# A planned decoder kernel: triangular inverses started from diagonal blocks of 32 rows instead of 16, with new GpSimd prices for the planner and an earlier load of the second token tile

## The chip, the cores and the metric

The kernel runs on one core of a Trainium2 chip. The metric is device time in microseconds (us) of one execution; lower is better. The kernel before was run three times: 1447.71, 1447.9 and 1452.22 us, median 1447.9 us.

## The reference, cut to what matters

One decoder layer in float32 over 32 sequences of 112 tokens and 256 features: a delta-rule attention block with its own gated MLP, a cross attention with 16 heads over 375 keys, and a mixture of six experts (two per token) plus a shared one. The change lies in the first of these. Its scan is

```python
def step(S, inp):                       # over the 112 tokens of a sequence
    q_t, k_t, v_t, b_t = inp
    Sk = jnp.einsum('bij,bj->bi', S, k_t)
    S = S + b_t[:, None, None] * (v_t - Sk)[:, :, None] * k_t[:, None, :]
    return S, jnp.einsum('bij,bj->bi', S, q_t)
```

Written without the loop, the scan of one sequence is a unit lower triangular system of 112 rows: its strictly lower part holds the products of keys, G = K K^T, with row s scaled by beta_s over the squared norm of key s. The kernel inverts that matrix and multiplies with the result.

## The kernel before, in words

**Groups.** The 32 sequences are worked on in eight groups of four (`GB = 4`), numbered 0 to 7. A group passes through three blocks. `delta_block(g)` and `queries(g)` form a long serial chain. It ends in the tile `qz`, which the group's cross attention needs. The cross attention is cut into 16 "quads" per group (`scores`, `turned`, `product`), each four heads of one sequence. `mixture_sparse(g)` then routes the group's tokens to the experts. The main loop issues the quads of group g one by one and puts between them pieces of the chain of group g + 1 (`main`), pieces of the mixture of group g - 1 (`others`), and the keys and values of the next sequence (`keys_values`). Group 0's chain has no quads to run beside; five steps of group 1's chain and the keys and values of the first two sequences are put into it. When group 7 begins, everything before is flushed, so instructions from either side are not mixed. At the end come 54 tiles of expert work (`sparse_tiles`), the last group's dense mixture, and `combine`, whose 56 row gathers are issued by GpSimd.

**The inverse.** For each of the four matrices of a group, `delta_block` computes G on TensorE, scales it into `W`, writes W to a DRAM table (`low`) and reads back the diagonal blocks of 16 rows, one block per partition (28 of them), as `L`. Forward substitution inverts these blocks: for j = 0 to 14, a product `part` = column j of L times row j of the inverse, and a subtraction from the rows below j. It runs on VectorE in group 0 and on GpSimd in all others (`plain = nc.vector if g == 0 else nc.gpsimd`). The inverted blocks and their transposes go back to two DRAM tables that hold zeros elsewhere, and are read as full 112 x 112 matrices `X` and `Y`. Three levels then double the block size (16 to 32, 32 to 64, 64 to 112). A level masks G (`C`, on GpSimd), multiplies C with X on TensorE (bank `pw`), scales the result to W on VectorE, and multiplies Y with W on TensorE (bank `px`, or `pyt` in the last level), which is subtracted from X. From the second level on Y is made again by transposing X on TensorE (bank `py`) with a copy on ScalarE.

**The order.** All calls go to a `Recorder`, which plans TensorE, VectorE and ScalarE by list scheduling. Each node has a price (`price`) and a number in program order. In the planner's clock, each engine takes the ready node with the lowest number, with a bonus for nodes that read a PSUM bank. A DMA ends a fixed time after its bytes have passed one common queue. The real engines then run in the planned order, each strictly in order, so a wrong price puts an instruction too early or too late in its queue. How many pieces of the chain go between two quads is set by `costs`, one entry for each `yield` of group 0's chain and at least 1.4 us each. PSUM banks (eight) and tile buffers (`qk`, `u`, `vs`, `a`, `G`, `A` exist once; `C` and `W` twice) bound how far work can be pulled forward.

**Names in the profile.** Every planned instruction is sent in line 381 and shows as L381, so tiles tell them apart. The substitution shows as POOL `W<-C,W` (product) and `W<-W` (subtraction); a level's matmuls as PE `X,C`, `W,Y`, `ident,X` and `Y,W`; the attention pieces as `kx,qz`, `ident,e` and `eT,vx`; the chain's MLP as `w_w_gate`, `w_w_up`, `w_w_down`; its last matmul as `w_xwqT`.

Of the kernel before, what the change touches and what calls it, by code (L numbers as in the profile page):

```python
# [15 lines left out]

P = 128
GB = 4
BS = 16
NEG = -1.0e9  # L20
BIG = 3.0e38

# [66 lines left out]
class Recorder:  # L89
# [53 lines left out]
    def price(self, name, op, outs, ins):  # L143
        n = max([self.length(a) for a in outs[:1] + ins] or [1])
        if name == "tensor":
            n = self.length(outs[0])
            return 0.123 if op == "transpose" else 2 * max(0.125, 0.02 + n / 1190)
        if name == "vector":
            if op == "tensor_tensor_reduce":
                return 0.62  # L150
            if op == "tensor_tensor_scan":
                return 0.37
            return max(0.18, 0.05 + n / 800)
        if name == "scalar":
            return 0.15 + n / 1400 + (0.18 if len(outs) > 1 else 0.0)
        if name == "gpsimd":
            return 0.97 if "dma" in op else 0.1 + n / 430
        return 0.08

    def note(self, name, op, args, kwargs):  # L160
# [92 lines left out]
    def flush(self, open_banks=()):  # L253
# [86 lines left out]
        while len(order) < len(nodes):  # L340
            best = None
            for e in self.clock:
                c = candidate(e)
                if c is not None and (best is None or (c[0], c[1].at) < (best[0], best[1].at)):
                    best = c
            if best is None:
                raise RuntimeError("no instruction can be issued")
            start, node = best
            e = node.eng
            for pile in (ready[e], future[e]):  # L350
                for entry in pile:
                    if entry[2] is node:
                        pile.remove(entry)
                        heapq.heapify(pile)
                        break
            node.start = start
            self.clock[e] = start + node.cost
            node.end = self.clock[e]
            if node.lag:
                self.moved = max(self.moved, node.end) + node.lag  # L360
                node.end = self.moved + 1.8
            for key in node.banks:
                self.free.sort()
# [22 lines left out]
def tile_decoder(ctx: ExitStack, tc: tile.TileContext, t: dict, out: bass.AP):  # L386
# [47 lines left out]
    blank = const.tile([T, D], F32, tag="blank", name="blank")  # L434
    nc.vector.memset(blank, 0.0)

    NB = GB * T // BS
    FAR = BS * T + BS
    blocks = [dram.tile([NB, FAR], F32, name=f"blocks_{i}") for i in range(3)]
    kept = [dram.tile([GB, T, D], F32, name=f"kept_{g}") for g in range(groups - 1)]  # L440


# [8 lines left out]


    levels = []
    s = BS
    while s < T:
        n = P // (2 * s)
        lv = const.tile([P, P], F32, tag=f"lv{s}", name=f"lv{s}")
# [26 lines left out]
    nothing = nothing[:T].rearrange("p c n -> p (c n)")[:, : NB * FAR // T]  # L484
    nc.vector.memset(nothing, 0.0)

    unit = const.tile([NB, BS, BS], F32, tag="unit", name="unit")
    nc.gpsimd.memset(unit, 0.0)
    nc.gpsimd.affine_select(
        out=unit, in_=unit, pattern=[[1, BS], [-1, BS]], compare_op=ALU.not_equal, fill=1.0, base=0,  # L490
        channel_multiplier=0,
    )
# [20 lines left out]
    for table in blocks[1:]:  # L513
        nc.gpsimd.dma_start(
            out=table.rearrange("n f -> (n f)").rearrange("(p q) -> p q", p=T), in_=nothing
        )
    nc.gpsimd.dma_start(out=rows[ZERO : ZERO + 1], in_=blank[:1])


# [69 lines left out]
    nc.gpsimd.tensor_tensor(nwb, nwb, wb, ALU.mult)  # L589
    keys_first, mask_first = load_keys(0), load_mask(0)  # L590
    xwk, xwv = weight("xwkT"), weight("xwvT")
    n2 = per_feature("norm2_w")
    wo = weight("Wo")
    w_gate, w_up, w_down = weight("w_gate"), weight("w_up"), weight("w_down")
    xwq, xwo = weight("xwqT"), weight("xwoT")
    keys_second, mask_second = load_keys(1), load_mask(1)
    x_second = load_x(1)
    gb = const.tile([T, NE], F32, tag="gb", name="gb")
    nc.sync.dma_start(out=gb, in_=t["gate_b"].partition_broadcast(T))
    w_route = weight("gate_wT")  # L600
# [92 lines left out]
    def delta_block(g, xt):  # L693
# [79 lines left out]

        W = dlt.tile([T, GB, T], F32, tag="W", name=f"W_{g}", bufs=2)
        plain.tensor_tensor(W, G, bcast(br2, T), ALU.mult)
        low, inv, turned_inv = blocks
        square = lambda m: m.rearrange("(b k) f -> b (k f)", b=GB)[:, : T * T].rearrange(
            "b (s t) -> s b t", s=T
        )
        diagonal = lambda m: m[:, : BS * T].rearrange("n (i t) -> n i t", t=T)[:, :, :BS]  # L780
# [4 lines left out]
        R = dlt.tile([NB, BS * BS + (BS // 2) ** 2], F32, tag="W", name=f"R_{g}", bufs=2)  # L785
        inverse = R[:, : BS * BS].rearrange("p (i j) -> p i j", j=BS)
        plain.tensor_copy(inverse, unit)
        for j in range(BS - 1):
            shape = [NB, BS - 1 - j, j + 1]
            part = R[:, BS * BS : BS * BS + shape[1] * shape[2]].rearrange("p (i j) -> p i j", j=j + 1)  # L790
# [12 lines left out]
        Y = dlt.tile([T, GB, T], F32, tag="Y", name=f"Y_{g}")  # L803
        nc.sync.dma_start(out=X, in_=square(inv))
        nc.sync.dma_start(out=Y, in_=square(turned_inv))
        yield
        yield

# [4 lines left out]
            nc.gpsimd.tensor_tensor(C, G, over_batches(levels[i][:T, :T]), ALU.mult)  # L813
            return C

        C = between_halves(0)
        for i in range(len(levels)):
            pw = bank("pw")
            for b in range(GB):
                matmul(pw[:T, b * T : (b + 1) * T], C[:, b, :], X[:, b, :], start=True, stop=True)  # L820
            W = dlt.tile([T, GB, T], F32, tag="W", name=f"W_{g}_{i}", bufs=2)
            nc.vector.tensor_tensor(W, pw[:T, :NT].rearrange("p (b t) -> p b t", b=GB), bcast(br2, T), ALU.mult)
            if i > 0:
                py = bank("py")
                for b in range(GB):
                    transpose(py[:T, b * T : (b + 1) * T], X[:, b, :], ident[:T, :T])
# [794 lines left out]
```

## Time and profile before

| | |
|---|---|
| median of three runs | 1447.9 us |
| the profiled execution: time, span | 1450.61 us, 1448.9 us |
| TensorE (PE) matmul busy | 1374.7 us, 95% |
| VectorE (DVE) busy | 966.8 us, 67% |
| ScalarE (ACT) busy | 701.3 us, 48% |
| GpSimd (POOL) busy | 305.4 us, 21% |
| mean granted TensorE clock | 0.98 |

A profile line of instructions gives engine, operation, output tile and inputs with their shapes, the count, the busy time, the mean duration of one in ns, and the idle time in front of them with what ended it. In the timeline view the first two columns are start and duration in us, and the bracket at the end is idle time before the instruction. In the view by windows each engine has busy us and a count; the column after POOL is the granted TensorE clock.

### The profile page before, as it was taken

How to read it: one execution, taken by the hardware profiler on the slowest of the kernel's cores; microseconds unless marked ns; L12 is line 12 of the kernel's file. 1: busy time of each engine (PE TensorE's matmuls, PEld its weight loads, DVE VectorE, ACT ScalarE, POOL GpSimd, SP SyncE). 2: the span in 40 equal slices, each digit the busy share in tenths (PEclk: the TensorE clock that was granted, in tenths of full speed). 3: DMA queues.
4: the chain of work that ended last, by engine and by line, in shares of the span. 5: the costliest groups of instructions: out<-in, count | busy, mean ns of one | idle time of the engine just before them, and what ended most of it. 6: DMA issues, size and time to landing. Idle time of an engine off the chain costs nothing.

```text
span 1448.9 us, 26826 instructions
## 1 busy us (share of the span) xinstructions
PE 1374.7 (95%) x9700; PEld 930.0 (64%) x9700; DVE 966.8 (67%) x3171; ACT 701.3 (48%) x1946; POOL 305.4 (21%) x477
## 2 busy tenths in 40 slices
PE   6679999999999989999999899989999999999988
PEld 4456766776577657765676567656766666666654
DVE  6645766865886488648765777577756875464566
ACT  2123756654665366536654565556556664222100
POOL 2121000311031103110311031203120032233175
PEclk9779999999999999999999999999999999999999
DMA  9100100113011301140104101310136022222254
GB/s 282 49 7 13 34 17 17 35 48 112 16 36 48 111 17 36 40 119 16 36 20 126 30 20 33 105 54 19 33 98 179 26 73 66 89 85 88 65 171 146
DMA packets 95076, 94.76 MB, mean 65 GB/s; under 512 B 29920, under 2 KB 89056, under 8 KB 94944
## 3 DMA queue, kind: packets, MB, share of 16 engines
q1 hardware_dynamic: 86816, 72.71, 17.3%
q0 software_dynamic: 8128, 20.34, 4.8%
q8 instruction: 77, 1.26, 0.4%
q14 instruction: 55, 0.45, 0.1%
HBM read 50.90 MB, written 42.12 MB: 64 GB/s over the span
## 4 chain that ended last, share of the span: by engine, by line
PE 67%; DVE 11%; DMA 6%; ACT 5%; POOL 5%; issue 4%; DVEq 0%; SPq 0%; ACTq 0%; POOLq 0%
PE bank L381 57%; PE bank L1327 6%; PE bank L1344 3%; POOL W L381 3%; ACT e L381 3%; DMA blocks<-W 2%; ACT eT L381 1%; DVE e L381 1%; DMA kept<-x 1%; DMA X<-blocks 1%; DVE W L381 1%; DVE mk L381 1%; DVE bst L381 1%; DMA x<-in_x_dram 1%; DVE rs_i L381 1%
## 5 line engine op out<-in xcount | busy, mean ns | idle before, releaser
L381 ACT ACTIVATE e<-e,nmx 112x375 f32<-112x375 f32 x512 | 306.3, 603 | 212.0 <-DVE nmx L381 211.8
L381 DVE CUSTOM_DVE_ANT_0 e<-bank,neg,flip 112x375 f32<-112x375 f32 x512 | 282.6, 603 | 33.7 <-PE bank L381 28.5
L381 ACT COPY eT<-bank 125x448 f32<-125x448 f32 x384 | 184.8, 529 | 86.2 <-PE bank L381 82.8
L381 PEld LDWEIGHTS bank<-ident,e 112*125 112x125 f32 x1536 | 187.8, 189 | 44.1 <-issue 10.6
L381 PE MATMUL bank<-ident,e 112*125 112x112 f32 x1536 | 207.2, 278 | 7.9 <-DVE nmx L381 4.9
L381 PE MATMUL bank<-kx,qz 32*112 32x375 f32 x1024 | 124.2, 519 | 0.0
L381 PEld LDWEIGHTS bank<-eT,vx 125*32 125x32 f32 x3072 | 68.9, 109 | 58.8 <-issue 40.6
L381 PE MATMUL bank<-eT,vx 125*32 125x112 f32 x3072 | 102.3, 264 | 4.2 <-ACT eT L381 3.9
L1327 PE MATMUL bank<-ew,xT 128*128 x216 | 101.9, 596 | 1.2 <-ACT xT L381 1.2
L381 PE MATMUL bank<-w_xwvT,cT 128*125 128x256 f32 x384 | 102.2, 393 | 0.0
L1144 POOL DMA_INDIRECT rows<-h,row_i x56 | 52.6, 939 | 223.3 <-DMA rows<-blank 118.2
L381 DVE SCALAR_TENSOR_TENSOR hs<-hs,bank 128x256 f32<-128x256 f32 x108 | 45.4, 421 | 79.5 <-ACT hs L381 77.5
L381 ACT ACTIVATION_READ_ACCUMULATOR e<-e,nmx 112x1 f32 x512 | 98.0, 191 | 0.0
L381 PE MATMUL bank<-cT,w_xwkT 128*128 128x375 f32 x256 | 95.4, 498 | 2.6 <-ACT eT L381 2.6
L381 POOL DMA_INDIRECT xg<-rows,take x54 | 51.5, 954 | 130.4 <-PE bank L381 121.4
L381 ACT ACTIVATE hs<-bank 128x256 f32<-128x256 f32 x54 | 20.7, 383 | 114.1 <-PE bank L1327 110.9
L381 PEld LDWEIGHTS bank<-w_xwvT,cT 128*125 128x125 f32 x384 | 67.3, 189 | 13.3 <-issue 5.6
L381 DVE SCALAR_TENSOR_TENSOR qk<-qk,bank 128x448 f32<-128x448 f32 x56 | 34.8, 621 | 57.5 <-ACT qk L381 49.8
L381 PEld LDWEIGHTS bank<-kx,qz 32*112 32x112 f32 x1024 | 43.3, 170 | 39.8 <-issue 15.6
L381 PEld LDWEIGHTS bank<-cT,w_xwkT 128*128 128x128 f32 x256 | 44.1, 190 | 38.1 <-ACT eT L381 6.2
L381 POOL TENSOR_TENSOR u<-h,nwb 112x1024 f32<-112x1024 f32 x7 | 16.9, 2408 | 215.8 <-issue 202.3
L381 DVE TENSOR_TENSOR x<-x,bank 112x512 f32<-112x512 f32 (+1 forms) x64 | 35.2, 549 | 36.0 <-PE bank L381 36.0
(245 smaller groups left out, 2405.0 us busy)
## 6 DMA issues: line engine op xcount, KB each, us to landing
rows<-blank SPq DMA_DIRECT2D x42, 448.0 KB
cT<-in_ctxT_dram SPq DMA_DIRECT2D x32, 375.0 KB
results<-y SPq DMA_DIRECT2D x54, 128.0 KB
mk<-in_mask_dram SPq DMA_DIRECT2D x32, 164.1 KB
x<-in_x_dram SPq DMA_DIRECT2D x7, 448.0 KB
kept<-x SPq DMA_DIRECT2D x7, 448.0 KB
out_dram<-x SPq DMA_DIRECT2D x4, 448.0 KB
blocks<-W SPq DMA_DIRECT2D x8, 196.0 KB
```

The source lines that it names most:

```text
L381: getattr(getattr(self.nc, name), op)(*[real(a) for a in args], **{k: real(v) for k, v in kwargs.items()})
L1144: sent = rec.nc.gpsimd.indirect_dma_start(out=rows[:], out_offset=bass.IndirectOffsetOnAxis(ap=where, axis=0), in_=row, in_offset=None)
L1327: rec.nc.tensor.matmul(p.real(), xT[:, c, :], w13[:, bass.ds(at[i] * (NC * 2 * MI) + c * 2 * MI, 2 * MI)], start=(c == 0), stop=(c == NC - 1),
L1344: rec.nc.tensor.matmul(p[:, :D].real(), hT[:, c, :], w2[:, bass.ds(at[i] * (CH * D) + c * D, D)], start=(c == 0), stop=(c == CH - 1),)
```

## The change

Groups 1 to 7 start from diagonal blocks of 32 rows: 16 blocks, one per partition, of which the last of each matrix is half empty. The substitution has 31 steps instead of 15, and the first of the three levels falls away. L takes the place of `qk`, the inverse that of `u`, the products that of `vs`. Three more DRAM tables are used, which are cleared by DMAs from the SP queue during group 0's chain. Group 0 keeps 16 rows and three levels. The substitution yields four times instead of twice in every group, and in groups 1 to 7 there are two more yields after it, while the missing level takes two away. The identity tile `unit` is replaced by two memsets. The planner's price of a GpSimd instruction goes from 0.1 + n/430 to 0.24 + n/476 us, of a GpSimd DMA from 0.97 to 1.24 us, with 2.6 us instead of 1.8 us to its end. The loads of the second keys, mask and token tile are issued ahead of seven other loads (`norm2_w`, `Wo`, the three MLP weights and the two attention weights).

```diff
-BS = 16
+SIZES = 16, 32
...
-            return 0.97 if "dma" in op else 0.1 + n / 430
+            return 1.24 if "dma" in op else 0.24 + n / 476
...
-                node.end = self.moved + 1.8
+                node.end = self.moved + (2.6 if node.eng == "POOL" else 1.8)
...
     xwk, xwv = weight("xwkT"), weight("xwvT")
+    keys_second, mask_second = load_keys(1), load_mask(1)
+    x_second = load_x(1)
     n2 = per_feature("norm2_w")
     wo = weight("Wo")
     w_gate, w_up, w_down = weight("w_gate"), weight("w_up"), weight("w_down")
     xwq, xwo = weight("xwqT"), weight("xwoT")
-    keys_second, mask_second = load_keys(1), load_mask(1)
-    x_second = load_x(1)
...
-        low, inv, turned_inv = blocks
+        size, n = SIZES[min(g, 1)], many[min(g, 1)]
+        low, inv, turned_inv = blocks[min(g, 1)]
...
-        L = dlt.tile([NB, BS, BS], F32, tag="C", name=f"L_{g}", bufs=2)
+        if g == 0:
+            L = dlt.tile([n, size, size], F32, tag="C", name=f"L_{g}", bufs=2)
+            spare = dlt.tile([n, size * size + (size // 2) ** 2], F32, tag="W", name=f"R_{g}", bufs=2)
+            flat, spare = spare[:, : size * size], spare[:, size * size :]
+        else:
+            L = qk.rearrange("p c n -> p (c n)")[:n, : size * size].rearrange("p (i j) -> p i j", j=size)
+            flat = dlt.tile([n, size * size], F32, tag="u", name=f"R_{g}")
+            spare = dlt.tile([n, (size // 2) ** 2], F32, tag="vs", name=f"part_{g}")
         nc.sync.dma_start(out=L, in_=diagonal(low))
         yield
-        plain.tensor_copy(inverse, unit)
-        for j in range(BS - 1):
-            shape = [NB, BS - 1 - j, j + 1]
+        plain.memset(flat, 0.0)
+        plain.memset(flat[:, :: size + 1], 1.0)
+        for j in range(size - 1):
+            shape = [n, size - 1 - j, j + 1]
...
-            if j in (4, 9):
+            if (j + 1) % (size // 4) == size // 8:
                 yield
...
+        first = min(g, 1)
+        for _ in range(2 * first):
+            yield
         yield
         yield
...
-        C = between_halves(0)
-        for i in range(len(levels)):
+        C = between_halves(first)
+        for i in range(first, len(levels)):
...
-            if i > 0:
+            if i > first:
                 py = bank("py")
...
-        for _ in range({5: 2, 6: 2, 7: 2, 8: 2, 9: 1, 11: 1, 18: 2}.get(i, 0)):
+        for _ in range({5: 2, 6: 2, 7: 1, 8: 1, 9: 1, 10: 1, 11: 1, 13: 1, 20: 2}.get(i, 0)):
             next(early_kv, None)
...
+        if i == 12:
+            for table in blocks[1]:
+                cleared(table, nc.sync)
+                rec.hold()
```

More of the change, by code (lines that the diff above doesn't have):

```diff
@@ L435, in tile_decoder @@
     nc.vector.memset(blank, 0.0)
-    NB = GB * T // BS
-    FAR = BS * T + BS
-    blocks = [dram.tile([NB, FAR], F32, name=f"blocks_{i}") for i in range(3)]
+    many = [GB * ((T + size - 1) // size) for size in SIZES]
+    blocks = [
+        [dram.tile([n, size * T + size], F32, name=f"blocks_{size}_{i}") for i in range(3)]
+        for n, size in zip(many, SIZES)
+    ]
     kept = [dram.tile([GB, T, D], F32, name=f"kept_{g}") for g in range(groups - 1)]
@@ L453, in tile_decoder @@
     levels = []
-    s = BS
+    s = SIZES[0]
     while s < T:
@@ L483, in tile_decoder, with cleared @@
     nothing = moe.at("hT", 0, [P, t["fc3T"].shape[0] // P, NT])
-    nothing = nothing[:T].rearrange("p c n -> p (c n)")[:, : NB * FAR // T]
+    nothing = nothing.rearrange("p c n -> p (c n)")
     nc.vector.memset(nothing, 0.0)
[L487 to L492, printed above, removed]
+    def cleared(table, queue):
+        n = table.shape[0] * table.shape[1]
+        p = next(p for p in range(P, 0, -1) if n % p == 0 and n // p <= nothing.shape[1])
+        flat = table.rearrange("n f -> (n f)").rearrange("(p q) -> p q", p=p)
+        queue.dma_start(out=flat, in_=nothing[:p, : n // p])
     head = const.tile([P, NE], F32, tag="head", name="head")
@@ L512, in tile_decoder @@
         nc.gpsimd.memset(vx[:, :, :, 1, :], 0.0)
[L513 to L516, printed above, removed]
+    for table in blocks[0][1:]:
+        cleared(table, nc.gpsimd)
     nc.gpsimd.dma_start(out=rows[ZERO : ZERO + 1], in_=blank[:1])
@@ L779, in delta_block @@
         )
-        diagonal = lambda m: m[:, : BS * T].rearrange("n (i t) -> n i t", t=T)[:, :, :BS]
+        diagonal = lambda m: m[:, : size * T].rearrange("n (i t) -> n i t", t=T)[:, :, :size]
         nc.sync.dma_start(out=square(low), in_=W)
-        L = dlt.tile([NB, BS, BS], F32, tag="C", name=f"L_{g}", bufs=2)
+        if g == 0:
[6 more added lines that the diff above has]
+            spare = dlt.tile([n, (size // 2) ** 2], F32, tag="vs", name=f"part_{g}")
         nc.sync.dma_start(out=L, in_=diagonal(low))
         yield
-        R = dlt.tile([NB, BS * BS + (BS // 2) ** 2], F32, tag="W", name=f"R_{g}", bufs=2)
-        inverse = R[:, : BS * BS].rearrange("p (i j) -> p i j", j=BS)
-        plain.tensor_copy(inverse, unit)
-        for j in range(BS - 1):
-            shape = [NB, BS - 1 - j, j + 1]
-            part = R[:, BS * BS : BS * BS + shape[1] * shape[2]].rearrange("p (i j) -> p i j", j=j + 1)
+        inverse = flat.rearrange("p (i j) -> p i j", j=size)
+        plain.memset(flat, 0.0)
+        plain.memset(flat[:, :: size + 1], 1.0)
+        for j in range(size - 1):
+            shape = [n, size - 1 - j, j + 1]
+            part = spare[:, : shape[1] * shape[2]].rearrange("p (i j) -> p i j", j=j + 1)
             to = inverse[:, j + 1 :, : j + 1]
```

## The prediction

> **What bounds the kernel now.** I read the page first (busy times, slices, chain), then the stretches of 10 us in which TensorE (PE) is not full, then the timeline of one group, from its first matmul to the next group's.
>
> ```profile
> PE 1374.7 (95%) x9700; PEld 930.0 (64%) x9700; DVE 966.8 (67%) x3171; ACT 701.3 (48%) x1946; POOL 305.4 (21%) x477
> ...
> PE   6679999999999989999999899989999999999988
> ...
> PEclk9779999999999999999999999999999999999999
> ...
> PE 67%; DVE 11%; DMA 6%; ACT 5%; POOL 5%; issue 4%; DVEq 0%; SPq 0%; ACTq 0%; POOLq 0%
> ```
>
> PE is busy for 1374.7 of 1448.9 us; 67% of the chain runs through it. It is idle for 74.2 us: by the stretches of 10 us, 31.8 before 110 us (slices 1 to 3), 12.0 after 1380, some 30 between. So a microsecond of PE work removed is a microsecond gained, unless idle time takes its place. Between 360 and 970 us the idle time sits where one group hands over to the next:
>
> ```profile
> 500.00:510.00 10.00, 8.99 (x48) 6.21 (x46) 4.73 (x20) 3.01 (x9) 0.00 (x0) 1.00 0.17 54
> 510.00:520.00 10.00, 8.14 (x66) 4.92 (x65) 9.31 (x41) 4.60 (x15) 0.00 (x0) 1.00 0.02 4
> 670.00:680.00 10.00, 8.41 (x55) 4.41 (x54) 8.04 (x18) 6.84 (x17) 2.39 (x1) 0.86 0.06 17
> ```
>
> In such a stretch PE has only the last quads left while the next group's chain ends in adds, a layernorm and `w_xwqT`. In the handover at 523 us the steps of the chain are: key projection from 384.7, W written at 408.3, blocks back at 412.65, substitution to 423.1, first level at 427.2, last `w_w_down` ended 506.3, `w_xwqT` 523.2, next group's scores 528.3.
>
> **The change, part by part.** *PE work.* The missing level takes out `X,C` and `W,Y` of one level, and one `ident,X`:
>
> ```profile
> 427.22 1.01 PE L381 MATMUL bank<-X,C 112*112 112x112 f32 x8 [0.20 <-DMA X<-blocks]
> ...
> 432.16 0.95 PE L381 MATMUL bank<-X,C 112*112 112x112 f32 x8
> 432.94 0.55 PE L381 MATMUL bank<-ident,X 112*112 112x112 f32 x4
> 433.33 1.04 PE L381 MATMUL bank<-ident,vo 128*112 128x128 f32 x8
> ```
>
> Start to start these are 0.85 (427.22 to 428.07), 0.86 for a `W,Y` (429.57 to 430.43) and 0.39 us, together 2.1 us in each of seven groups: -14.7 us. The level's VectorE work (0.62 + 0.60 us), GpSimd mask (1.14) and ScalarE copy (0.53) lie beside PE; I count them at nothing.
>
> *The substitution.* Fifteen steps on 28 partitions now:
>
> ```profile
> 412.65 0.21 POOL L381 TENSOR_TENSOR W<-C,W 28x15 f32<-28x15 f32 x1 [4.31 <-DMA C<-blocks]
> ...
> 417.80 0.31 POOL L381 TENSOR_TENSOR W<-W 28x64 f32<-28x64 f32 x1
> ...
> 422.89 0.21 POOL L381 TENSOR_TENSOR W<-W 28x15 f32<-28x15 f32 x1
> 423.16 0.60 POOL L381 COPY C<-W 28x256 f32<-28x256 f32 x1
> ```
>
> ```profile
> L381 POOL TENSOR_TENSOR C<-G,lv 112x448 f32<-112x448 f32 x24 | 27.2, 1135 | 68.6 <-DMA blocks<-C 25.3 <-DVE ss L381 24.7 <-PE bank L381 18.7
> ...
> L381 POOL TENSOR_TENSOR u<-h,nwb 112x1024 f32<-112x1024 f32 x7 | 16.9, 2408 | 215.8 <-issue 202.3 <-ACT h L381 13.6
> ...
> L381 POOL TENSOR_TENSOR W<-W 28x64 f32<-28x64 f32 x7 | 2.2, 309 | 0.6
> ```
>
> The two long forms differ by 576 elements and 1273 ns: 2.2 ns an element, 0.145 us fixed (the 28x64 row sits 0.02 above that, so I take 0.165). Starts lie 0.075 us beyond the end before. Check on 16 rows: 30 x (0.165 + 0.075) + 1360 elements x 2.2 ns = 10.2 us; the timeline has 10.45. For 32 rows there are 62 instructions, and the sum of (31 - j)(j + 1) is 5456 elements, twice: 62 x 0.24 + 10912 x 0.0022 = 38.9 us. The two memsets come while GpSimd waits for the blocks. The transposing copy (0.6 us for 256 elements, so up to 2.4 for 1024) delays Y alone, which is needed a level step later. So X comes 28.5 us later, less the missing level (432.16 - 427.22 = 4.9): **the chain is 23.6 us late** from there on.
>
> *Who waits.* Nothing but this chain needs the inverse at once; quads, keys, values and mixture go on. In the 28 us in which PE used to do levels and output products for the chain, about 16 us of other work is pulled forward, and there are that many fewer fillers later. The chain can catch up where it waits now though its input is there: `w_w_gate` and `w_w_down` start at 479.85, 488.69, 494.74 and 502.66, after ends at 472.3, 482.9, 491.7 and 498.4 (20.6 us), and the norm before them takes 6 us longer than its instructions. That is 27 us of slack against 23.6. The planner gives a late node precedence, as its number is low, and the four extra yields move the chain's later pieces back by about two quads. When PE has nothing else, the next group's projections (9.6 us; their tile `qk` is free after 506) and the mixture can come earlier. I take 1 us more idle time at each of six handovers.
>
> *The granted clock.* A handover bubble costs more than itself:
>
> ```profile
> 676.84 4.94 PE L381 MATMUL bank<-nT,w_Wk 128*128 128x448 f32 x8 [1.48 <-DVE nT L381]
> 681.61 3.17 PE L381 MATMUL bank<-nT,w_Wq 128*128 128x448 f32 x8
> ```
>
> After 1.48 us without work the same projection takes 4.94 instead of 3.25 us (at 384.71), the granted clock being 0.86 in this stretch: 1.7 us more. [...] I take two more such falls: 3.4 us. So handovers cost 6 + 3.4 = +9.4 us, by the rule +6.
>
> *GpSimd beside VectorE.* [...]
>
> ```profile
> L381 DVE COPY mk<-rs x32: 293/294/2510, 152.0 to 1231.3; 112x256 f32<-112x256 f32 x32
> ```
>
> The 2510 ns is at 527.8 us, while `u<-h,nwb` runs. But between 412.65 and 423 us the 14 two-input instructions of VectorE take 0.15 to 0.30 us where 0.16 is usual, 0.27 us too much in all. [...] By the nearest row, the substitution itself, it is 1 to 2 us on an engine that is 67% busy: I take nothing, and keep 3 us per group for the slow end. GpSimd's queue has the add to `x` (453.3) and eight scatters (462 to 489) behind; the substitution ends at about 452 (group 2's times), so it passes none of them, unless the mixture is pulled forward: then up to 8 x 1.23 us.
>
> *The start.* PE idles 4.15 us before 43.89 and 5.6 us before 62.69. VectorE starts group 0's substitution at 50.44, though its blocks were asked for at 40.93 and, at group 1's 4.3 us, are there by about 45: the planned order puts group 1's layernorm, projections and sums first. VectorE never waited for the second token tile (its first `bst` at 37.6 follows without a gap), so the earlier load ends no wait by itself; it acts only by letting the planner place that layernorm earlier. That can give 5 to 6 us. Against it: group 1's levels no longer fill the handover at 121 to 128 us (3.5 us of matmuls), and three clears of 231 KB (0.7 MB, 2 us at the 330 GB/s of this stretch) may stand on SP ahead of W's write. The seven loads moved back land 3 us later and are first used at 86.9; hidden by more than 40 us. I take 0, with -6 and +6 as ends.
>
> *The tail.* GpSimd issues 56 gathers at 1.23 us each; the old price was 0.97, so VectorE's queue holds the sums that need them too early, and the dense mixture behind them waits:
>
> ```profile
> 1408.46 6.19 PE L381 MATMUL bank<-ew,hT 128*112 128x256 f32 x14 [3.55 <-DVE hT L381]
> ...
> 1440.35 3.28 PE L381 MATMUL bank<-w_fc3T,hT 128*112 128x256 f32 x14 [1.69 <-DVE hT L381]
> ```
>
> With 0.83 and 0.62 earlier these are 6.7 us. The price of 1.24 cures that, but the last gather (1437.8, 2.7 us to land) and its store end about 3.5 us before the kernel does: -3 us. The new price of other GpSimd work (1.18 for a mask that takes 1.135) changes little.
>
> **Sum:** -14.7 + 9.4 + 0 - 3 = -8.3 us against the profiled execution's 1450.6 (span and 1.7 us around it). That execution is 2.7 us above the median of the runs; the same difference on 1447.9 gives 1440.
>
> **Rivals.** *(1) The chain sets the period.* If the slack cannot all be used (each step also waits for an engine in the middle of another piece), quads and fillers are used up and PE stands. Place: before `w_xwqT` in six handovers, worst at 1108, where the flush lets nothing of the next group in. It decides from 3 us more per handover (18 against 17.7). At 4 us and a clock fall at every second: 24 + 5 - 17.7 = +11, 1459. For it: 27 against 23.6 is thin. Against it: the front of the next chain can move up by 20 us.
> *(2) The gain is eaten.* Idle time grows by about what PE saves: 1448.
> *(3) The start pays too.* The substitution of group 0 moves up and nothing is lost at 121 us: -8.3 - 6, and somewhat more if handovers do not grow: 1432. Against it: the lost cover.
> *That the change does not do what it says:* for the early loads this is my own case (no wait was theirs); the level does fall away.
>
> **How the numbers follow.** My forecast has 0.46, (3) 0.13, (2) 0.15, (1) 0.26. About 0.3%, 4.3 us, is what a measurement can tell here. So faster 0.59, same 0.15, slower 0.26. The range runs from (3) with its end, 1427, to (1), 1459; the unknown 3 us per group of contention lies within its upper end.
>
> **What would show it.** Right: 62 GpSimd instructions of 39 us in all per group; PE busy about 15 us less; `w_xwqT` of group 3 no later than about 523 us; PE idle between 110 and 1380 us below 42 us; no PE wait above 1.5 us on `hT` after 1380. Wrong: that idle time near 60 us and PE waiting for `X` or `h` before `w_xwqT`; VectorE's mean of 603 ns for the score instruction or 163 ns for `rs_u` risen; a first level of group 0 no earlier than 62.7 us speaks against (3).

## The result, and the profile after

The kernel before takes 1447.9 us, the changed one 1531.3 us (medians of four runs each on one chip; 1529.8 to 1535.4 for the changed one): **ratio 1.0573, 95% interval 1.0543 to 1.0603, slower**. The prediction said 1440 and at most 1459. The page of the changed kernel, with the lines that answer to those shown of before:

```profile
PE 1365.7 (89%) x9560; PEld 922.7 (60%) x9560; DVE 986.3 (64%) x3158; ACT 698.5 (46%) x1939; POOL 479.8 (31%) x699
...
PE   7687999996999599949995999779999999999996
...
PEclk9788999997999799969998999989999999999998
...
PE 55%; DMA 14%; POOL 14%; DVE 9%; issue 4%; ACT 2%; SPq 1%; POOLq 0%; DVEq 0%; ACTq 0%
```

TensorE does 9 us less, but its idle time is 165.1 us (1530.8 span less 1365.7) instead of 74.2. Five times, in slices 10, 14, 18, 22 and 26 to 27, TensorE falls to 4, 5, 6 or 7 tenths, and the granted clock falls with it. The chain of waits now has 14% in DMA and 14 in GpSimd, where it had 6 and 5. The windows, chosen at the low slices, show stands of the whole core (stretches in which hardly anything runs):

```profile
340.00:355.00 15.00, 1.84 (x8) 0.91 (x6) 0.00 (x0) 1.23 (x3) 1.86 (x2) 0.68 0.60 181
500.00:510.00 10.00, 0.00 (x0) 0.00 (x0) 0.00 (x0) 0.00 (x0) 1.86 (x2) 0.62 0.54 156
670.00:680.00 10.00, 0.00 (x0) 0.00 (x0) 0.00 (x0) 0.00 (x0) 0.00 (x0) 0.50 0.68 200
```

From 500 to 510 us no matmul, no VectorE and no ScalarE instruction runs, only transfers (share 0.54) and GpSimd's issue of two of them. What the engines wait for, from the view of waits between 240 and 1080 us (total, times, longest):

```profile
PE bank L381 <- DVE vo L381: 88.9, 5, 20.3
...
DVE bst L381 <- DMA x<-in_x_dram: 98.0, 5, 22.1
```

TensorE waits five times for VectorE's copy `vo`, and VectorE waits five times for the token tile `x`. The timeline of VectorE and of TensorE's `w_Wo` at the second stand shows how these hang together:

```profile
495.36 1.95 PE L381 MATMUL bank<-A,u 112*128 112x112 f32 x16
...
496.45 0.62 DVE L381 COPY vo<-bank 128x448 f32<-128x448 f32 x1 [1.95 <-PE bank L381]
517.38 0.43 DVE L381 BATCH_NORM_STATS2 bst<-x 112x6 f32<-112x256 f32 x1 [20.31 <-DMA x<-in_x_dram]
517.73 0.61 DVE L381 COPY vo<-bank 128x448 f32<-128x448 f32 x1
...
518.39 5.50 PE L381 MATMUL bank<-w_Wo,vo 128*112 128x256 f32 x14 [18.50 <-DVE vo L381]
```

The two `vo` copies take the chain's own output product (group 3) out of PSUM. Between them VectorE's planned queue holds the first layernorm instruction of group 4, whose token tile has not come. The second copy's matmuls (`A,u`) end at 497.31 us, yet it runs only at 517.73, behind the layernorm's wait of 20.31 us. `w_Wo` waits 18.50 us for it, and every other engine runs dry. In the kernel before the same three instructions stand like this:

```profile
447.21 0.62 DVE L381 COPY vo<-bank 128x448 f32<-128x448 f32 x1
448.11 0.62 DVE L381 COPY vo<-bank 128x448 f32<-128x448 f32 x1 [0.27 <-PE bank L381]
...
505.43 0.43 DVE L381 BATCH_NORM_STATS2 bst<-x 112x6 f32<-112x256 f32 x1 [5.07 <-DMA x<-in_x_dram]
```

There the layernorm reached the head of the queue (500.36 us) 51.6 us behind the second copy's end, and waited 5.07 us. The wait existed, with the chain's copies long done; what it cost there is tested below. Why the tile comes when it does shows in GpSimd's and SP's queues:

```profile
472.10 0.24 POOL L381 TENSOR_TENSOR u<-u,vs 16x31 f32<-16x31 f32 x1
472.40 1.99 POOL L381 COPY qk<-u 16x1024 f32<-16x1024 f32 x1
474.56 0.99 POOL L1156 DMA_INDIRECT rows<-h,row_i  x1 [0.17 <-issue]
...
486.07 0.93 POOL L1156 DMA_INDIRECT rows<-h,row_i  x1 [9.28 <-DMA rows<-blank]
...
503.20 0.93 POOL L1156 DMA_INDIRECT rows<-h,row_i  x1 [6.83 <-DMA rows<-blank]
```

```profile
479.93 1.23 SPq L381 DMA_DIRECT2D rows<-blank  x2
489.82 9.49 SPq L381 DMA_DIRECT2D rows<-blank  x2
...
506.95 1.22 SPq L381 DMA_DIRECT2D rows<-blank  x2
508.26 1.14 SPq L381 DMA_DIRECT2D kept<-x  x1
...
513.71 0.31 SPq L381 DMA_DIRECT2D x<-in_x_dram  x1
```

The mixture's eight scatters of group 1's tokens (POOL, `rows<-h`) and SP's six clears of group 2's places (`rows<-blank`) write one DRAM tile and take turns, each waiting for the other's transfer (between 240 and 1080 us SP's queue waits 126.7 us in all for scatters, GpSimd 110.5 us for clears). The store `kept<-x` and the load `x<-in_x_dram` stand behind the clears in SP's queue. The taking of turns is not new: before, the clears ran from 465.85 and the load was issued at 502.01. Nor did the change make the load later: in the first of these handovers it was issued at 352.27 us, before at 355.56. What is later is the chain: its first `vo` copy comes 102.4 us behind the start of group 1's `w_xwqT` (338.41 - 235.98) instead of 73.9 (302.62 - 228.68).

The loss by stretches. From group 1's `w_xwqT` to group 7's ("the stretch" below) before took 879.2 us and the changed kernel 953.9: **+74.7**. To group 1's `w_xwqT` it lost 7.3 us (235.98 against 228.68). From group 7's to the end it is 341.0 against 341.1.

### The profile page after: what moved, and what is told of

The parts are those of the page before. It is cut to its first block, busy times and chain, and to the rows that moved or that the text cites. A ratio compares the mean times of both kernels' runs of the same rounds, so it can differ in the third digit from the quotient of the medians.

```text
span 1530.8 us, 26763 instructions
## 1 busy us (share of the span) xinstructions
PE 1365.7 (89%) x9560; PEld 922.7 (60%) x9560; DVE 986.3 (64%) x3158; ACT 698.5 (46%) x1939; POOL 479.8 (31%) x699
## 4 chain that ended last, share of the span: by engine, by line
PE 55%; DMA 14%; POOL 14%; DVE 9%; issue 4%; ACT 2%; SPq 1%; POOLq 0%; DVEq 0%; ACTq 0%
PE bank L381 46%; PE bank L1339 6%; POOL u L381 6%; POOL vs L381 5%; DMA rows<-h,row_i 4%; DMA rows<-blank 4%; PE bank L1356 3%; DMA kept<-x 2%; DVE e L381 2%; POOL rows L1156 1%; DMA x<-in_x_dram 1%; DVE rs_u L381 1%; ACT e L381 1%; DVE rs_i L381 1%; ACT h L381 1%
## 5 line engine op out<-in xcount | busy, mean ns | idle before, releaser
L381 PE MATMUL bank<-ident,e 112*125 112x112 f32 x1536 | 203.5, 277 | 4.3 <-DVE nmx L381 1.7
L381 POOL TENSOR_TENSOR vs<-qk,u 16x31 f32<-16x31 f32 (+15 forms) x217 | 109.3, 504 | 50.8 <-DMA qk<-blocks 34.3
L381 PE MATMUL bank<-w_Wo,vo 128*112 128x256 f32 x128 | 42.5, 498 | 88.9 <-DVE vo L381 88.9
L381 POOL TENSOR_TENSOR u<-u,vs 16x31 f32<-16x31 f32 (+15 forms) x217 | 116.0, 534 | 17.0
L381 DVE BATCH_NORM_STATS2 bst<-x 112x6 f32<-112x256 f32 x96 | 38.6, 407 | 98.9 <-DMA x<-in_x_dram 98.2
L381 PEld LDWEIGHTS bank<-eT,vx 125*32 125x32 f32 x3072 | 69.2, 109 | 47.8 <-issue 31.2
L381 PEld LDWEIGHTS bank<-w_Wo,vo 128*112 128x112 f32 x128 | 30.0, 240 | 100.6 <-DVE vo L381 91.0
L381 POOL TENSOR_TENSOR C<-G,ident 112x448 f32<-112x448 f32 x7 | 8.0, 1138 | 256.4 <-ACT G L381 256.4
```

The lines of the kernel that those rows point to most:

```text
L381: getattr(getattr(self.nc, name), op)(*[real(a) for a in args], **{k: real(v) for k, v in kwargs.items()})
```

## The experiments

Theory A says that VectorE's planned order does the harm; theory B, that the clears and scatters make the load late; rival 1, that the long chain costs the time by itself; rival 2, that the new prices reordered the queue. "The waits for x" are those of VectorE's layernorm for the token tile. A form without the clears has no time: two thirds of the table of routed rows would hold no numbers. The runs fell on more than one chip: the kernel before took 1494.2, 1489.4, 1448.7, 1454.7 and 1492.5 us beside the five sets. Ratios are within a set. The stretch is compared across sets: with 16 rows it was 833.8 and 833.0 us on two chips, which differed in the tail (last section).

| kernel | stretch, us | VectorE's waits for x (total, longest) | ratio to before, 95% interval |
|---|---|---|---|
| before | 879.2 | 21.5, 5.1 | 1 |
| changed | 953.9 | 98.0, 22.1 | 1.0573 (1.0543 to 1.0603) |
| layernorm held back | 905.4 | none | 1.0200 (1.0180 to 1.0221) |
| changed, old prices | 926.8 | 44.6, 12.7 | 1.0343 (1.0315 to 1.0372) |
| before, new prices | 853.8 | none | 0.9815 (0.9799 to 0.9832) |
| changed, clears independent | 881.6 | none | 1.0052 (1.0032 to 1.0072) |
| changed, 16 rows | 833.8 | none | 0.9785 (0.9761 to 0.9810) |
| 11 of 31 steps | 856.7 | none | 0.9824 (0.9795 to 0.9853) |
| 21 of 31 steps | 858.1 | 3.6, 1.5 | 0.9874 (0.9845 to 0.9902) |
| 26 of 31 steps | 894.3 | 33.2, 8.0 | 1.0164 (1.0129 to 1.0200) |
| held back and independent | 899.6 | none | 1.0184 (1.0143 to 1.0225) |
| before, clears independent | 858.9 | none | 0.9909 (0.9875 to 0.9944) |
| 16 rows, one set of tables | 833.0 | none | 0.9717 (0.9683 to 0.9750) |
| 11 steps, no extra yields | 838.4 | none | 0.9712 (0.9676 to 0.9748) |
| no extra yields | 961.7 | 120.7, 24.9 | 1.0519 (1.0480 to 1.0558) |
| no extra yields, independent | 886.1 | 1.3, 0.7 | 1.0021 (1.0004 to 1.0037) |

**The layernorm held back.** The planner may place group g + 2's layernorm only behind the chain's last layernorm of group g + 1.

```diff
...
+        mark = len(rec.nodes)
         layernorm(a, xt, h)
+        if g > 1:
+            for node in rec.nodes[mark:]:
+                node.before[normed_of[g - 1].at] = normed_of[g - 1]
...
         layernorm(a2, xt)
+        normed_of[g] = rec.nodes[-1]
...
```

> The changed kernel, with one thing more for the planner: the layernorm of group g + 2 may not be planned before the last instruction of the layernorm in queries(g + 1). Theory A (VectorE's planned order puts that layernorm, which waits for a token load that lands late, in front of the chain's own copies, and everything stands): VectorE's wait for x<-in_x_dram falls from 98 us to under 15, PE's wait on vo from 89 us to under 10, time 1440 to 1460. Rival 1 (the 39 us substitution makes the chain itself too long for the period): the stands move elsewhere, time above 1490. Rival 2 (the clear and scatter queue alone sets the period): the load is as late as before and group g + 2 starts late, time above 1490.

Stretch 905.4. VectorE's waits for x and TensorE's for `vo` are gone, and 48.5 of the 74.7 us with them. The planned place of the layernorm did carry that part. The time fell short of theory A, which had at most 1460, 1.008 of before: it is 1.020. Against 16 rows with the same prices (853.8) 51.6 us are still lost.

**The prices, both ways.** The changed kernel with the old GpSimd prices, and the kernel before with the new ones:

```diff
-            return 1.24 if "dma" in op else 0.24 + n / 476
+            return 0.97 if "dma" in op else 0.1 + n / 430
...
-                node.end = self.moved + (2.6 if node.eng == "POOL" else 1.8)
+                node.end = self.moved + 1.8
```

> The changed kernel with the old GpSimd prices and DMA lag in the planner. If the new prices moved the layernorm to the front (rival 2), the time falls to about 1450. If the blocks of 32 rows did it (theories A and B), it stays between 1500 and 1560: the plan still has the substitution at over 28 us (62 x 0.1 + 10912/430 = 31.6) and the chain about as late.

> The kernel before with the new GpSimd prices and DMA lag alone. Theories A and B: within 6 us of 1448, with the waits of the dense mixture after 1380 us shorter by some 4 us (end 1 to 3 us earlier). If prices were the cause: above 1490.

With 16 rows the new prices take 25.4 us off the stretch, and the waits for x are gone: a gain of 1.85% that the change carried with it, and that neither side of the expectation had. The second handover, before and with the new prices:

```profile
462.04 0.98 POOL L1144 DMA_INDIRECT rows<-h,row_i  x1 [6.42 <-DVE row_i L381]
...
502.01 0.33 SPq L381 DMA_DIRECT2D x<-in_x_dram  x1
```

```profile
449.15 0.98 POOL L1144 DMA_INDIRECT rows<-h,row_i  x1 [6.69 <-DVE row_i L381]
...
489.92 0.33 SPq L381 DMA_DIRECT2D x<-in_x_dram  x1
```

The layernorm's turn is where it was (124.0 us behind the start of group 2's `w_xwqT`, 123.7 before). The scatters start earlier, and with them the clears, the store and the load.

With 32 rows the new prices are worse than the old (953.9 against 926.8), and here they do move the layernorm. With the old ones its turn in the second handover comes 12.9 us behind the second `vo` copy (493.98 to 506.83), with the new ones ahead of it. So rival 2 holds for that order. It is not the whole loss: with the old prices 47.6 us are lost to before, though the waits for x are half as long. Of the rest, TensorE waits 13.7 us for `X` itself.

**Clears and scatters independent.** They write different rows when the scatter belongs to an earlier group, so the dependency between them can be declared away; the planned order stays as it was.

```diff
+        def clear():
+            sent = rec.nc.sync.dma_start(out=to, in_=of)
+            for i, other in placed:
+                if i // GB < g:
+                    tc.declare_no_dep(sent.ins, other.ins, reason="they write different rows")
+            wiped.append((g, sent))
...
+            for group, other in wiped:
+                if group > i // GB:
+                    tc.declare_no_dep(sent.ins, other.ins, reason="they write different rows")
```

> The changed kernel, in which the clears of a group's rows and the scatters of earlier groups are declared independent, as they write different rows; the planned order is untouched. Theory B (late load: clears and scatters take turns on the two queues, about 40 us, and the store of kept x and the load of the token tile stand behind them) expects the turns to fall away: eight scatters in about 10 us, the load issued some 20 us earlier, the five stands of 20 us gone, stretch from group 1's to group 7's w_xwqT 953.9 -> 850 to 900. Theory A alone (VectorE's planned order puts the layernorm of the group after next ahead of the chain's own copies, whatever the queues do) expects the wait for x to shrink only by a few us and the stretch to stay above 925. Rival 1 (the chain of 39 us is too long by itself) expects the wait for x to go and other waits to take its place, as with the layernorm held back: about 905.

Stretch 881.6, 72.3 of the 74.7 us. The second handover, GpSimd's last two scatters, SP's queue and VectorE:

```profile
467.73 0.93 POOL L1163 DMA_INDIRECT rows<-h,row_i  x1 [0.30 <-issue]
468.96 0.93 POOL L1163 DMA_INDIRECT rows<-h,row_i  x1 [0.30 <-issue]
```

```profile
481.08 0.31 SPq L381 DMA_DIRECT2D kept<-x  x1
481.48 0.44 SPq L381 DMA_DIRECT2D mk<-in_mask_dram  x1
484.52 0.31 SPq L381 DMA_DIRECT2D x<-in_x_dram  x1
```

```profile
488.59 0.62 DVE L381 COPY vo<-bank 128x448 f32<-128x448 f32 x1 [1.95 <-PE bank L381]
489.13 0.42 DVE L381 BATCH_NORM_STATS2 bst<-x 112x6 f32<-112x256 f32 x1
489.49 0.62 DVE L381 COPY vo<-bank 128x448 f32<-128x448 f32 x1
```

The eight scatters take 8.7 us from first to last issue (29.9 in the changed kernel). The layernorm still stands between the two `vo` copies, and costs nothing, as its tile is there. So the stand needs both: the order of A and the late load of B; taking away either ends it, and B is the cheaper cure.

**Before, with the clears independent.** The same edit in the kernel before, with its old prices.

> The kernel before (old prices, 16 rows), with clears and scatters of different groups declared independent. It has five waits of VectorE for the token tile of up to 5.1 us (21.5 us in all). If these are the same mechanism at small size, and what the new prices removed (stretch 879.2 -> 853.8), the stretch falls by 15 to 25 us, to 855 to 864, and the waits for x are gone. If the prices acted by another way, it stays above 870. Time on this chip 0.98 to 0.99 of before in the first case.

Stretch 858.9, waits for x gone. So the 5 us waits of the kernel before were this mechanism at a small size. It cost that kernel about 20 us of the stretch (13 us of the whole time; group 1's `w_xwqT` came 4.2 us later). The new prices bring 25.4 us, and the same waits are gone there; whether the two gains add up was not tried.

**Both cures in the changed kernel.**

> The changed kernel with both: the layernorm of the group after next held behind the chain's own last layernorm, and clears and scatters of different groups declared independent. If the late load was what made the early place of that layernorm harmful, holding it back has nothing left to gain once the load comes early: 881.6 of the independent form or worse, up to the 905.4 of the held form. If order and queue each cost something of their own, it falls below both, to about 860.

899.6: holding the layernorm back has nothing left to gain once the load is early, and costs 18 us.

**Sixteen rows, all other edits kept.**

```diff
-SIZES = 16, 32
+SIZES = 16, 16
...
-        first = min(g, 1)
+        first = 0
```

> The changed kernel with blocks of 16 rows and three levels in every group; all other edits stay (prices, load order, clears at the start, four yields in the substitution, tiles shared with qk, u and vs). If the 32 rows are the whole cost, the stretch from group 1's to group 7's w_xwqT is that of the kernel before with the new prices, 854, and the time about 1466 on this chip, 0.98 of before. If the sharing of qk, u and vs or the yields cost something (the chain of the next group cannot start its projections until the substitution of this one is done), it is 870 to 900.

833.8, lower than either case expected. Going back to 16 rows takes away more than the whole loss: the rest of the change is a gain, though TensorE waited 21.5 us for the first `X` at the start.

So this form, not the kernel before, is what the 32 rows must be held against: they cost 120.1 us of the stretch. With the clears independent 47.8 of these stay, though no wait for x is left. The stretch of that form, and of this one:

```profile
235.88:1117.45 881.57, 845.51 (x6532) 579.48 (x6528) 623.27 (x2049) 490.96 (x1364) 308.55 (x474) 0.98 0.13 37
```

```profile
246.77:1080.52 833.75, 832.02 (x6653) 584.78 (x6649) 596.09 (x2058) 492.75 (x1366) 160.38 (x288) 1.00 0.20 57
```

TensorE is idle for 36.1 us against 1.7, in gaps of at most 3.7 us, and its clock is 0.98 instead of 1.00. Taking the two extra yields away as well does not lower it (886.1, see below). So this part goes with the 32 rows themselves, as rival 1 had it; by which way, no run separates.

**How many steps.** In groups 1 to 7 only a part of the 31 steps is done, so the inverse is incomplete. The edit for 11; the others keep `j % 3 != 1` (21) and `j % 6 != 1` (26):

```diff
+            if g == 0 or j % 3 == 0:
                 plain.tensor_tensor(part, ..., ALU.mult)
                 plain.tensor_tensor(to, to, part, ALU.subtract)
```

> The changed kernel with only every third of the 31 steps of the substitution in groups 1 to 7 (work left out: the inverse is incomplete): 22 instructions, estimated 13.3 us instead of 38.9, so the chain is 2 us earlier than with 16 rows and a level more. If the length of the substitution is the cause (lateness, in whatever way it acts), the stretch from group 1's to group 7's w_xwqT comes out at 854 less six levels of 2.1 us, about 841. If something else in the 32-row path costs the time (the tiles, the order, three levels become two), it stays above 880.

> The changed kernel with 21 of the 31 steps of the substitution in groups 1 to 7 (work left out: the inverse is incomplete): 42 instructions, estimated 26.1 us; the chain is about 11 us late. A loss that grows step by step with the length (slack used up evenly) puts the stretch at the middle, about 895. A threshold (27 us of slack, as the prediction had it: nothing lost until it is used up) puts it near 841 to 850. A switch in the planned order (the layernorm placed ahead of the chain's copies once the chain is late enough) puts it at either end, with the wait of VectorE for the token tile either absent or above 15 us in each group.

> The changed kernel with 26 of the 31 steps of the substitution in groups 1 to 7 (work left out: the inverse is incomplete): 52 instructions, estimated 32.5 us, so the chain is about 17 us late. It places the threshold between 26.1 us (stretch 858.1, no wait for x above 1.5 us) and 38.9 us (953.9, waits of 20 us). If the store of kept x and the load of x are late by what the scatters are late, and VectorE's layernorm waits from the moment at which that exceeds its margin, the wait for x should be about 38.9 - 32.5 = 6.4 us shorter than the full one, some 14 us in each of five handovers, stretch 915 to 930. If the planner still finds room (slack of 27 us, the prediction's figure, would be enough for 17), it stays at 858 to 865.

856.7, 858.1, 894.3, and 953.9 with all: nothing is lost between an estimated 13 and 26 us, then 36 us for the next 6.4 and 60 for the last 6.4. That is a threshold. Three sizes missed: 11 steps lie above the 841 expected, and at 26 steps the waits (8.0 us at most) and the stretch are lower than the expectation had them. The same place of the second handover with 21 and with 26 steps:

```profile
465.35 0.62 DVE L381 COPY vo<-bank 128x448 f32<-128x448 f32 x1 [0.27 <-PE bank L381]
...
489.82 0.43 DVE L381 BATCH_NORM_STATS2 bst<-x 112x6 f32<-112x256 f32 x1 [0.62 <-DMA x<-in_x_dram]
```

```profile
482.38 0.62 DVE L381 COPY vo<-bank 128x448 f32<-128x448 f32 x1
...
501.84 0.43 DVE L381 BATCH_NORM_STATS2 bst<-x 112x6 f32<-112x256 f32 x1 [6.24 <-DMA x<-in_x_dram]
```

From the end of the second `vo` copy to the layernorm's turn (its start less its wait) there are 51.6 us before, 23.2 with 21 steps, 12.6 with 26; with all 31 the layernorm is ahead of that copy. The chain slides back towards an instruction that waits for memory, until it lies behind it.

**The two extra yields.** With 11 steps the period of a group (mean of the five from group 2's `w_xwqT` to group 7's) was 142.2 us, with 16 rows and a level more 138.6. Windows of 10 us behind the substitution, 11 steps:

```profile
699.00:709.00 10.00, 8.81 (x86) 6.07 (x87) 9.53 (x28) 6.28 (x18) 8.75 (x17) 0.99 0.01 2
709.00:719.00 10.00, 10.00 (x53) 8.00 (x53) 5.65 (x18) 4.06 (x12) 2.03 (x2) 0.66 0.33 73
```

In the first window TensorE is idle for 1.19 us in pieces of 0.7 and less; in the second the mean granted clock is 0.66. The experiment takes away the two yields after the substitution:

```diff
-        for _ in range(2 * first):
-            yield
         yield
         yield
```

> The changed kernel with every third of the 31 steps only (work left out: the inverse is incomplete) and without the two extra yields after the substitution. With the yields and this short substitution the period of a group was 142.2 us, where 16 rows and a level more gave 138.8 and the level saves 2.1; the 5.5 us too many are some 2.4 us of TensorE's idle time and a clock fall to 0.66 in the 10 us after the substitution. If the two yields (no piece of the chain issued between two quads, so fewer fillers) make these gaps, the period falls to 137 to 139 and the stretch to 825 to 835. If the gaps come from the missing level's matmuls, which filled that place, or from the tiles, it stays at 141 to 143.

Period 138.9, stretch 838.4: the yields cost 18.3 us there, and from its fourth slice on the clock's digit is 9 throughout. The level that fell away still shows no gain: 16 rows have 138.6. TensorE's idle time in the stretch (7.6 us against 1.7) is a part of it. At full length the yields matter differently:

> The changed kernel at full length (31 steps, 38.9 us) without the two extra yields after the substitution; nothing else is changed. If length and yields add up to the lateness, the chain's later pieces come about two places of the main loop (some 17 us) earlier, as if the substitution took 22 us: no wait of VectorE for the token tile above 2 us, stretch from group 1's to group 7's w_xwqT 840 to 865, 0.975 to 0.99 of before. If the length alone makes the stands (the pieces after X wait for X whatever place they have), the waits stay above 12 us in each of five handovers, and the stretch above 920.

> The same, and clears and scatters of different groups declared independent. With 39 us and the yields that took the stretch from 953.9 to 881.6. If the stands are gone without the yields already, it gains little here (0 to 8 us); if they are still there, it takes them away, to about 865, 0.985 of before.

```profile
DVE bst L381 <- DMA x<-in_x_dram: 120.7, 5, 24.9
```

961.7 and 886.1 against 953.9 and 881.6 with the yields: I had expected the yields to be half of the lateness, and that falls. The stands come with the length of the substitution, with these yields or without. Without the yields TensorE waits 96.6 us for `nmx` in place of `vo`: another instruction behind the same layernorm.

**A version that beats both.** The changed kernel with 16 rows everywhere and the one set of tables of the kernel before:

```diff
-        for n, size in zip(many, SIZES)
-    ]
+        for n, size in zip(many[:1], SIZES[:1])
+    ] * 2
...
-        if i == 12:
-            for table in blocks[1]:
-                cleared(table, nc.sync)
-                rec.hold()
```

> The best version by the runs so far: the changed kernel with 16 rows in all groups (ratio 0.9785 when it had a second set of tables), now with the one set of tables of the kernel before, so that the three clears on SP during group 0's chain fall away. In that run TensorE waited 21.5 us for X of group 0, and its first w_xwqT came at 142.3 us instead of 131.3. If the clears made that wait, it comes at 125 to 131 here, and group 7's w_xwqT at 1065 to 1072 instead of 1080.5; five periods of 139 us stay as they are. If work had only been moved from the start into the later stretch, group 7's stays near 1080. Time 0.970 to 0.979 of before.

```profile
PE 1353.3 (96%) x9700; PEld 928.0 (66%) x9700; DVE 957.4 (68%) x3172; ACT 702.1 (50%) x1946; POOL 306.1 (22%) x482
...
PE   6679999999999999999999999999999999999996
...
PEclk9779999999999999999999999999999999999999
```

1408.0 us against 1448.7 beside it. The first `w_xwqT` comes at 127.9 us (142.3 with the second set of tables), group 7's at 1065.4. No slice between the start and the end falls below 9. Prices, load order, the four yields within the substitution, the shared tiles, the memsets and the new places of the first keys and values are its edits; of these only the prices were tried alone (group 7's `w_xwqT` at 1083.0). Which of the others brings the further 17.6 us was not separated.

## Why the prediction was wrong

**The step that failed** is "Who waits". It set 27 us of slack against 23.6 us of lateness and took "1 us more idle time at each of six handovers". The slack was real: up to an estimated 26 us of substitution nothing is lost. But it ended before 23.6. At 21 steps, which by the prediction's own working are 10.7 us late (26.1 - 10.45 - 4.94), it still held; at 26 steps, 17.1 us late, it was gone. And the price beyond it was 20 us at each of five handovers, not 1. I had looked for what waits for the inverse, and had not followed VectorE's queue: which instruction with a DMA behind it comes next after the chain's own, and how far behind. The wait for x stood in the trace of before (5.07 us at 505.43). It is in no term of the sum.

The stands are not all: beside 16 rows in the same kernel the 32 rows cost 120.1 us, of which the independent clears take back 72.3. The other 47.8 us, idle time in small gaps and a lower clock, stand against the +9.4 us that the sum has for the handovers, and their cause stays open.

**The queues.** The prediction named the eight scatters behind the substitution and stopped at "it passes none of them". The first scatter does come 2.2 us behind the end of the last subtraction (472.34 to 474.56). But the queue that decides is SP's: clears, store and load behind the scatters. Freed of the taking of turns, the changed kernel wins 72.3 us.

**The substitution** was right: 38.9 us worked out, 37.1 measured (435.27 to 472.34), and 1.99 us for the copy against "up to 2.4". The lateness came out somewhat larger: 28.5 us at the `vo` copies of the first handover against 23.6.

**PE work.** `X,C` went from 192 to 136 matmuls, `W,Y` from 128 to 72, `ident,X` from 64 to 36, as said. The gain of 14.7 us is not seen as time anywhere: with 11 steps and no extra yields, where nothing stands, the period is that of 16 rows with the level. Some 6 us of idle time in the stretch take its place there; the rest stays open.

**The clock.** Two more falls were counted. There were five, one for each stand (mean granted clock 0.68 from 340 to 355 us, 0.62 from 500 to 510, 0.50 from 670 to 680 and from 830 to 840, 0.53 from 990 to 1000), and others behind small gaps (a mean of 0.66 over 10 us with 11 steps). The kind was right, the number followed from the wrong step. The row at 676.84 us does not show what sets off a fall, nor that a handover always costs more than its gap: in the trace of before the same projection waited 1.48, 1.50, 1.48 and 1.50 us at 384.71, 531.31, 676.84 and 827.30 us, and took 3.25, 3.25, 4.94 and 4.93 us. The 1.7 us for each of two falls were an estimate from one of the two slow rows. The +6 named beside +9.4 is the handovers without any fall, and no run shows it.

**The prices** were counted for the tail alone (-3 us). They took 25.4 us off the stretch with 16 rows, where the scatters and the load behind them came earlier, and with 32 rows they put the layernorm ahead of the chain's copy. The prediction had seen that the prices place VectorE's work in its queue, and had asked so only of the gathers.

**GpSimd beside VectorE.** VectorE's busy time grew by 19.5 us, 2.8 a group. But the missing level took 8.5 us of VectorE's work away, so what is left grew by about 28 us, 4 a group, beyond the 3 us kept for the slow end. The score instruction stayed at 602 ns (603), `rs_u<-rs_i` went from 165 to 176 ns. The 3 us were an estimate; no run shows what made the rest longer, or isolates what it cost.

**Start and tail.** The first `w_xwqT` came 1.3 us earlier (predicted 0, -6 to +6), although group 0's first level started 4.1 us earlier (58.6 against 62.7): TensorE then waited 7.18 us for `h` of group 0, in the place where the prediction expected the lost cover of group 1's levels. The tail was 0.1 us shorter (predicted 3).

**The rivals.** Rival (1), that the chain sets the period, was the right side. It was priced at 4 us a handover and placed before `w_xwqT`; the stand is at `w_Wo`, 20 us long. It "decides from 3 us more per handover" by its own rule, so with the wait for x followed it should have had the larger chance.

## What to carry to other kernels

Where engines run a planned order strictly in order, find in each queue the next instruction that waits for a transfer, and measure how far behind the critical chain's own instructions it stands. That distance told more here than the idle time of the chain: with 21 steps it was 23.2 us and nothing was lost, with 26 it was 12.6 and 36 us were. With a critical instruction behind the transfer nearly the whole wait was paid (five waits, 98.0 us in all; 95.8 us more than with 21 steps). A wide distance is no proof of safety: at 51.6 us, in the kernel before, waits of up to 5.1 us still cost 20. Follow such a transfer back through every queue to what it stands behind, and look for dependencies that are only of the tile and not of the rows: here they cost the kernel before 20 us of the stretch and the changed one 72. When several edits come together, run each alone: the other edits together were a gain of 2.15% that the 32 rows hid.

## What the runs showed of the hardware

During the stands of the changed kernel the mean granted clock was 0.50 to 0.68 over 10 to 15 us. With 11 steps, gaps of 0.2 to 0.7 us between 695 and 709 us were followed by a mean of 0.66 from 709 to 719. In the kernel before, a gap of 1.50 us that ended at 531.31 us was followed by no fall: 1.00 from 530 to 540.

Two chips gave nearly the same program different tails. With 16 rows, the stretch was 833.8 us with the second set of tables and 833.0 with the one set, on another chip; from group 7's `w_xwqT` to the end it was 375.4 and 340.1, though the edit puts no instruction there. All traced kernels beside the slower runs of before had 374.8 to 383.7 there, beside the faster ones 340.1 to 344.8. In the slow tail (375.4 us, 16 rows) VectorE waits in the last sums of gathered rows for something that the trace puts to no queue of this core (32.2 us in all), and TensorE has 5.80 us of work in 30:

```profile
DVE x L381 <- remote: 32.2, 3, 18.7
```

```profile
1370.00:1400.00 30.00, 5.80 (x16) 2.66 (x14) 2.68 (x6) 0.54 (x1) 19.36 (x21) 0.66 0.35 101
```

The traces of before, of the changed kernel and of the best version, all with fast tails, show no such wait. What differs between the chips was not found. The kernel before took 1448.7 us on one and 1494.2 on another, so a time is compared here only with that of before beside it on the same chip.
